# Pairs 2 to 15 of blocks in tiles of 32 rows by 64 columns, with operands gathered at half width

## The chip, the cores and the metric

The kernel runs on one core of a Trainium2 chip. The time is device microseconds of one execution: 732.87 us, the median of three runs (732.12 to 734.15). Everything is float32.

The core's engines work side by side and wait for each other by semaphores: TensorE (PE; its weight loads are shown apart as PEld), VectorE (DVE), ScalarE (ACT), GpSimd (POOL) and SyncE (SP). Here POOL does no arithmetic in the main loop: it issues indirect DMAs (gathers), whose descriptors it writes itself. SP issues plain DMAs.

## What is computed

Three layers of a compressed interaction network over x of shape (1024, 39, 64), as (sample b, field, position e):

```python
def _cin_layer(Xk, X0, W, b):
    O = W.shape[0]
    Hk, Fdim = (Xk.shape[1], X0.shape[1])
    Wr = W.reshape(O, Hk, Fdim)
    return jnp.einsum('bhe,bfe,ohf->boe', Xk, X0, Wr) + b[None, :, None]
...
for W, b in ((W0, b0), (W1, b1), (W2, b2)):
    Xk = _cin_layer(Xk, X0, W, b)
    outs.append(Xk.sum(axis=-1))
cin_output = jnp.concatenate(outs, axis=-1)
return cin_output @ fc_w.T + fc_b
```

Only a sum over e and one final number per sample are wanted. So the kernel needs, for every column (b, e), two sets of 64 values that are both sums over pairs of fields: the first layer, and a second one whose weights come from W1, W2 and fc_w. Their product, summed over e, and terms that are linear in the fields give the answer.

## The kernel before

**Blocks and pairs.** The 1024 samples are 32 blocks of 32 samples, that is 2048 columns of 64 positions each. Two blocks are a pair (0 to 15), as they share one set of short operands. In a block the 780 pairs of fields become rows of products: six chunks of 128 rows (PAIRS, NPAIR = 6), and 32 rows more, the square step, which serves four column quarters (1024 columns wide, four groups of 32 partitions).

**Gathers (POOL).** Both operands of a product are gathered by field from a table in DRAM: xd, three of them (NTAB = 3), each with the two blocks of a pair, 40 rows a block. roll(n), L178 to L181, fills rt[n % 2], five tiles of 128 x 2048, by five indirect DMAs (gather_rows, L173 to L176) with a list of rows; roll_small fills ut and vt (128 x 1024) for the pair. load(n), L166 to L171, brings block n of x into its table. Most loads are issued by SP; those of blocks 4 and 5 by POOL, in its queue between the gathers.

**Products (DVE).** product(n, c) multiplies two tiles of rt elementwise into p, 128 x 2048. The pool of p has four buffers, and the loop makes the product of step at + 4 (AHEAD) while step at is multiplied, so DVE can start one as soon as TensorE has finished the step four before it.

**Matmuls (PE).** multiply(n, c), L555 to L565, takes the 128 columns of weights wa for chunk c against the four quarters of p (512 columns), into four PSUM banks. A float32 matmul is two instructions in the profile. join(n), L567 to L596, does the square rows and the linear terms of both blocks as tiles of 32 rows by 64 columns of weights, eight of which work in the array at once: 16 for the square, 8 for the linear terms.

**Finish.** When a block's banks are complete, ACT copies one half of each with a bias (z), DVE multiplies it with the other half into g (L609), and DVE sums g over e (L620). ACT has copied the 39 field rows into g before (fields, L598).

**Order.** It is written by hand. A pair has 13 steps: six chunks, the join, six chunks. The text counts them through: pair 0 is steps 0 to 12 (6 is its join), pair 1 is 13 to 25, pair 2 begins at 26. roll(n + 2) stands behind the last product of block n, so a pair's tiles are gathered while the pair before it runs.

## Time and profile before

| | us |
|---|---|
| median of three runs | 732.87 |
| span of the profiled execution | 731.4 |
| first product matmul (L559) from the span's start | 17.1 |
| 32 blocks of six chunks, 16 joins on TensorE | L559 x1536, L579 x512, L590 x256 |

The profile was taken of one execution. Its rows give the engine, the line of the kernel, the operation, what it writes and reads (out<-in), the shape, how often, and then busy time and mean length; behind the second bar stands the idle time of the engine just before them and what ended it. A timeline row begins with the start and the length in us. "Issue" means that the profile shows nothing that was waited for. Matmuls are pipelined: an instruction's length is more than its distance from the next one.

### The profile page before, as it was taken

To read this page: it belongs to the slowest core of one execution; us is meant where nothing else is said; L and a number is where in the kernel's file an instruction comes from. 1 tells how busy PE (TensorE), PEld (TensorE's weight loads), DVE (VectorE), ACT (ScalarE), POOL (GpSimd) and SP (SyncE) were. 2 spreads that over 40 slices of the span, in tenths; PEclk is the share of its full clock that TensorE was granted. 3 is DMA by queue.
4 is the path that set the end of the run, shared out by engine and by line. 5 is a ranking of instruction groups with operands and counts; after the bars stand their busy time and mean duration, and the time that the engine had idled before them with its cause. 6 is when DMAs were issued, how large, how long until landed. Compare 5 with 4: busy or idle time off the path is not lost.

```text
span 731.4 us, 6351 instructions
## 1 busy us (share of the span) xinstructions
PE 724.7 (99%) x2375; PEld 316.1 (43%) x2375; DVE 638.3 (87%) x521; ACT 166.9 (23%) x240; POOL 397.6 (54%) x254
## 2 busy tenths in 40 slices
PE   8999999999999999999999999999999999999998
PEld 4444444444444444444444444444444444444443
DVE  6999798988889988889988889888898988889885
ACT  3332121222212222221222212222121221212222
POOL 6789886536555445754537555455654547545300
PEclk9999999999999999999999999999999999999999
DMA  8997899789575887757679675896767777565700
GB/s 268 376 337 280 315 342 356 290 307 338 232 273 231 281 336 286 270 225 285 269 288 330 223 289 219 304 348 236 268 256 274 301 287 266 224 252 236 288 0 0
DMA packets 65983, 197.24 MB, mean 270 GB/s; under 512 B 40110, under 2 KB 40179, under 8 KB 45984
## 3 DMA queue, kind: packets, MB, share of 16 engines
q0 software_dynamic: 28784, 185.56, 65.5%
q1 hardware_dynamic: 35468, 9.29, 5.5%
q10 hardware_dynamic: 1700, 1.99, 1.0%
q8 instruction: 18, 0.29, 0.1%
q14 instruction: 13, 0.11, 0.0%
HBM read 196.76 MB, written 10.60 MB: 284 GB/s over the span
## 4 chain that ended last, share of the span: by engine, by line
PE 99%; DVE 0%; DMA 0%; issue 0%; ACT 0%; DVEq 0%
PE po L559 91%; PE po L579 4%; PE po L590 2%; PE idle L279 0%; PE pv L406 0%; PE pt L487 0%; PE small L323 0%; PE pv L487 0%; PE pw L418 0%; DMA fcrow<-in_fc_w 0%; PE tr L543 0%; DVE g L609 0%; DVE pairs L526 0%; DVE sums L631 0%; ACT z L607 0%
## 5 line engine op out<-in xcount | busy, mean ns | idle before, releaser
L559 PE MATMUL po<-p,wa 128*128 128x512 f32 x1536 | 666.0, 594 | 0.0
L219 DVE TENSOR_TENSOR p<-r 128x2048 f32<-128x2048 f32 (+2 forms) x198 | 434.1, 2224 | 72.4 <-PE po L559 67.1
L559 PEld LDWEIGHTS po<-p,wa 128*128 128x128 f32 x1536 | 290.5, 190 | 371.7 <-issue 354.6
L174 POOL DMA_INDIRECT r<-xd,lists x156 | 302.3, 1938 | 267.1 <-issue 266.2
L607 ACT ACTIVATE z<-po,columns 64x512 f32<-64x512 f32 x128 | 87.3, 682 | 380.1 <-PE po L590 217.9
L609 DVE SCALAR_TENSOR_TENSOR g<-po,b0s,z 64x512 f32<-64x512 f32 x128 | 95.9, 749 | 9.3 <-ACT z L607 5.3
L602 ACT COPY g<-r 39x1024 f32<-39x1024 f32 x64 | 66.7, 1043 | 155.0 <-DVE sums L620 126.8
L620 DVE TENSOR_REDUCE sums<-g 103x16 f32<-103x1024 f32 x62 | 75.6, 1220 | 2.1
L174 POOL DMA_INDIRECT u<-xd,lists x16 | 38.9, 2432 | 7.5 <-issue 4.6
L174 POOL DMA_INDIRECT v<-xd,lists x16 | 38.5, 2403 | 4.9 <-issue 4.9
L579 PE MATMUL po<-p,wa 32*64 32x512 f32 x512 | 31.6, 600 | 0.0
L221 DVE TENSOR_TENSOR p<-u,v 128x1024 f32<-128x1024 f32 x16 | 19.5, 1218 | 0.0
L579 PEld LDWEIGHTS po<-p,wa 32*64 32x64 f32 x512 | 9.4, 131 | 20.2 <-issue 19.4
L590 PE MATMUL po<-u,wa 32*64 32x512 f32 x256 | 17.0, 587 | 0.0
L174 POOL DMA_INDIRECT r<-xh,lists x8 | 8.0, 996 | 4.8 <-DVE tmp L387 2.7
L590 PEld LDWEIGHTS po<-u,wa 32*64 32x64 f32 x256 | 5.7, 132 | 8.0 <-issue 8.0
L526 DVE TENSOR_TENSOR pairs<-both 128x2 f32<-128x2 f32 (+27 forms) x59 | 6.1, 171 | 0.2
L544 ACT COPY wa<-tr 128x128 f32<-128x128 f32 x8 | 2.1, 266 | 16.2 <-PE tr L543 16.2
L279 PE MATMUL idle<-const-float32-1.0 128*128 128x256 f32 (+1 forms) x8 | 4.0, 596 | 0.8 <-PEq L793 0.8
L543 PE MATMUL tr<-unit,pairs 128*128 128x128 f32 x8 | 2.4, 294 | 2.2 <-DVE pairs L526 2.2
L543 PEld LDWEIGHTS tr<-unit,pairs 128*128 128x128 f32 x8 | 1.2, 151 | 4.7 <-ACT pairs L524 2.7
L168 POOL DMA_DIRECT2D xd<-in_x x3 | 3.2, 1055 | 0.0
(97 smaller groups left out, 56.7 us busy)
## 6 DMA issues: line engine op xcount, KB each, us to landing
xd<-in_x SPq DMA_DIRECT2D x28, 312.0 KB
r<-xd,lists POOLq DMA_INDIRECT x156, 8.9
xd<-in_x POOLq DMA_DIRECT2D x3, 312.0 KB, 7.6
w2s<-in_w ACTq DMA_DIRECT2D x1, 624.0 KB
w1s<-in_w ACTq DMA_DIRECT2D x1, 624.0 KB
w0s<-in_w0t ACTq DMA_DIRECT2D x1, 380.2 KB
xh<-in_x ACTq DMA_DIRECT2D x2, 156.0 KB
xd<-xh SPq DMA_DIRECT2D x2, 156.0 KB
```

The source lines that it names most:

```text
L174: nc.gpsimd.indirect_dma_start(dst, None, table, bass.IndirectOffsetOnAxis(ap=lists[:, k : k + 1], axis=0))
L219: nc.vector.tensor_tensor(p[:, cols], r[:, i, cols], r[:, k, cols], ALU.mult)
L221: nc.vector.tensor_tensor(p[:, 0:SUB], ut[n // 2 % 2], vt[n // 2 % 2], ALU.mult)
L279: nc.tensor.matmul(idle[:, 0:cols], nc.const_aps.tensor(1.0, (128, 128), F32), nc.const_aps.tensor(1.0, (128, cols), F32), start=True, sto ...
L526: nc.vector.tensor_tensor(out, diagonal(a, b, sa, sb), diagonal(b, a, sb, sa), ALU.add)
L559: nc.tensor.matmul(po[n][m], wa[:, c, side : side + 2 * H], p[:, bass.ts(m, MM)], start=n % 2 == 0 and c == 0, stop=n % 2 == 1 and c == NP ...
L579: nc.tensor.matmul(dst[half * H : half * H + H], wa[rows, NPAIR, at : at + H], p[rows, bass.ts(side, MM)], start=t >= 2, stop=t < 2 and ha ...
L590: nc.tensor.matmul(dst[half : half + H], wa[rows, NPAIR + 1, H : 2 * H], ut[n // 2 % 2][rows, bass.ts(side, MM)], start=False, stop=t < 2,)
L602: nc.scalar.copy(gt[H : H + F], rt[n % 2][0:F, 0, bass.ts(m, SUB)])
L607: nc.scalar.activation(z[one], po[n][m][other], AF.Identity, bias=fc0s[other])
L609: return lambda: nc.vector.scalar_tensor_tensor(g[n][m // 2][0:H, at], po[n][m][one], b0s[one], z[one], ALU.add, ALU.mult)
L620: nc.vector.tensor_reduce(sums[:, b_at : b_at + SB], g[n][m // 2].rearrange("p (b e) -> p b e", e=E), AX.X, ALU.add,)
```

## The change

Pair 0 and pair 15 stay as they are. In pairs 1 to 14 all products and matmuls are arranged in parts t = 0 to 3:

- A part holds 32 rows of the 128 of each operand, for all four half-blocks of the pair: partitions 32 s to 32 s + 31 hold half-block s (block s // 2, half s % 2). roll_part(k, t) gathers it into half of an rt tile: five indirect DMAs of 128 x 1024, with the lists in narrow. A pair has 20 of these where it had 10 of 128 x 2048; u and v stay. The order of release is part by part: part t of pair k + 1 is gathered behind the last product of part t of pair k.
- part_product makes 2048 columns at a time: two chunks at once from 1024 columns (whole), or four or two chunks of one side, a side being one of the two 512-column quarters of the half-blocks (side, both).
- part_multiply multiplies each unit of 512 columns with 4 x 2 tiles of 32 rows by 64 columns. Row group s needs the weights of rows 32 t to 32 t + 31, so wn holds wa's rows moved to the other partitions (part_weights, twelve ACT copies during pair 0).
- A side has four banks, one for each half-block. Side 0 is complete in the middle of the last step but one of a pair and is opened again with the next pair's first step; part_finish frees the banks, and the sums follow in the next pair.
- The fields come to g by four DMAs of SP a pair (part_fields) instead of ACT copies.

The core of the diff:

```diff
+TILES = 4
+ROWS = 128 // TILES
+NPART = NBLK // 2
...
+    def roll_part(k, t):
+        table = xd[k % NTAB].rearrange("f (t c) -> (f t) c", c=SUB)
+        for i in range(NT):
+            nc.gpsimd.indirect_dma_start(
+                part(t)[:, i],
+                None,
+                table,
+                bass.IndirectOffsetOnAxis(ap=narrow[:, t, i : i + 1], axis=0),
+            )
...
+    def part_multiply(k, t, units, p, last):
+        for u, (c, side) in enumerate(units):
+            begin = open_part(k, side)
+            end = last and not any(s == side for _, s in units[u + 1 :]) and last[side]
+            for s in range(TILES):
+                rows = slice(ROWS * s, ROWS * s + ROWS)
+                w = wa[rows, c] if s == t or c == NPAIR else wn[rows, c, t]
+                for half in range(2):
+                    at = ((s + side) % 2 + half) * H
+                    nc.tensor.matmul(
+                        po[2 * k + side][s][half * H : half * H + H],
+                        w[:, at : at + H],
+                        p[rows, bass.ts(u, MM)],
+                        start=begin,
+                        stop=bool(end),
+                    )
...
+    def part_steps(k):
+        found = []
+        for t in range(TILES):
+            if t in (0, TILES - 1):
+                if t:
+                    found.append((k, t, "square", 0))
+                found += [(k, t, "side", 0), (k, t, "both", 0), (k, t, "side", 1)]
+            else:
+                found += [(k, t, "whole", at) for at in range(3)]
+        return found
+
+    WHOLE = (0, NPART - 1)
     steps = []
-    for n in range(0, NBLK, 2):
-        steps += [(n, c) for c in range(NPAIR + 1)] + [(n + 1, c) for c in range(NPAIR)]
...
+    for k in range(NPART):
+        steps += whole_steps(k) if k in WHOLE else part_steps(k)
...
-            if c == NPAIR - 1 and n + 2 < NBLK:
-                roll(n + 2)
+            k = n // 2 + 1
+            if c == NPAIR - 1 and k < NPART:
                 if n % 2 == 0:
-                    roll_small(n + 2)
-                if n < 2:
-                    load(n + 4, nc.gpsimd)
+                    roll_part(k, 0)
+                    roll_small(2 * k)
+                    roll_part(k, 1)
+                else:
+                    roll_part(k, 2)
+                    roll_part(k, 3)
+                load(n + 4, nc.gpsimd)
...
+        p[step], units_of[step] = part_product(t, kind, which)
+        done = which == (2 if kind == "whole" else 1) and k + 1 < NPART
+        if done and k + 1 not in WHOLE:
+            roll_part(k + 1, t)
+        elif done and t % 2:
+            roll(2 * k + 2 + t // 2)
+        if done and t == 1:
+            roll_small(2 * k + 2)
```

Three places of the built programs show what moves. On TensorE, the end of pair 0 and a whole pair read like this before (L559 is multiply, L579 and L590 are join):

```order
L559 MATMUL po<-p,wa 128x512
L579 MATMUL po<-p,wa 64x512 x16
L590 MATMUL po<-u_86,wa 64x512 x8
L559 MATMUL po<-p,wa 128x512 x48
L579 MATMUL po<-p,wa 64x512 x16
```

The change has this around the square of pair 1 (L633 is part_multiply, L646 the linear terms):

```order
L633 MATMUL po<-p,wa 64x512 x2
L633 MATMUL po<-p,wn 64x512 x6
L633 MATMUL po<-p,wa 64x512 x2
L633 MATMUL po<-p,wn 64x512 x2
L633 MATMUL po<-p,wa 64x512 x16
L646 MATMUL po<-u_91,wa 64x512 x8
L633 MATMUL po<-p,wn 64x512 x6
L633 MATMUL po<-p,wa 64x512 x2
```

Small tiles stand on both sides of the square, so the array keeps one shape from step 13 to the end of pair 14.

On POOL, these are the gathers of pair 1 and the first of pair 2 before (xd_69 is pair 1's table, xd_70 pair 2's, and the rows that write xd_70 are the loads of blocks 4 and 5):

```order
L174 DMA r_84<-xd_69,lists 128x2048 x5
L174 DMA u_87<-xd_69,lists 128x1024
L174 DMA v_89<-xd_69,lists 128x1024
L168 DMA xd_70<-in_x 1248x1x64
L174 DMA r_85<-xd_69,lists 128x2048 x5
L168 DMA xd_70<-in_x 1248x1x64
L174 DMA r_84<-xd_70,lists 128x2048 x5
```

In the change they are:

```order
L145 DMA r_88<-xd_69,narrow 128x1024 x5
L130 DMA u_91<-xd_69,lists 128x1024
L130 DMA v_93<-xd_69,lists 128x1024
L145 DMA r_88<-xd_69,narrow 128x1024 x5
L124 DMA xd_70<-in_x 1248x1x64
L145 DMA r_89<-xd_69,narrow 128x1024 x10
L124 DMA xd_70<-in_x 1248x1x64
L145 DMA r_88<-xd_70,narrow 128x1024 x10
```

The second load has 12 gathers of pair 1 and the first load ahead of it before the change, and 22 gathers and the first load after it. A part's gather reads rows of both blocks, so the last row shown waits for both loads, where the first gathers of pair 2 had needed one.

On DVE, from the last products of pair 1 to the finish of its side 0, the change has (p are products; those from r1_89 are of pair 1's part 3, those from r0_88 of pair 2's part 0; the rows of L697 free the banks of pair 1's side 0):

```order
L221 TENSOR_TENSOR p_909<-r1_89 128x2x2x512
L212 TENSOR_TENSOR p_943<-r1_89 128x2048
L212 TENSOR_TENSOR p_974<-r0_88 128x2048
L221 TENSOR_TENSOR p_1008<-r0_88 128x2x2x512
L697 SCALAR_TENSOR_TENSOR pairs_97<-po_611,b0s_79,z_1042 64x512
L697 SCALAR_TENSOR_TENSOR pairs_97<-po_612,b0s_79,z_1042 64x512
L697 SCALAR_TENSOR_TENSOR both_96<-po_613,b0s_79,z_1043 64x512
L697 SCALAR_TENSOR_TENSOR both_96<-po_614,b0s_79,z_1043 64x512
L212 TENSOR_TENSOR p_1052<-r0_88 128x2048
```

Before, the finish of a block stood between products too, but its banks were not opened again for six steps; here two products of the next pair stand ahead of the operations that free the banks with which that pair begins.

More of the change, by code (lines that the diff above doesn't have):

```diff
@@ L291, in cin_kernel @@
         wide = prep.tile([128, 5, NT], F32, name="wide")
-        fields_of = prep.tile([128, NT], F32, name="fields_of")
         used = [0]
@@ L379, in cin_kernel @@
             )
-        r, most, seat, far = (new() for _ in range(4))
+        r, most, far = (new() for _ in range(3))
         both_of = prep.tile([128, 2], F32, name="both_of")
@@ L687, in cin_kernel, with whole_step @@
         multiply(n, c, p[n, c], (1,))
-    for at, (n, c) in enumerate(steps[:-TAIL]):
-        if c == 0 and 2 <= n and n + 4 < NBLK:
-            load(n + 4)
+    units_of = {}
+    sums_due = []
+    def whole_step(at, n, c):
         quarters = range(BLK // MM)
@@ L716, in cin_kernel, with part_step @@
                 spread(k)
-        if at - 1 in over:
-            finish(over[at - 1])
-            fields(over[at - 1] + 1)
-        if at + AHEAD < len(steps):
-            n, c = steps[at + AHEAD]
-            if at + AHEAD <= NPAIR:
+    def part_step(k, t, kind, which):
+        tile_ = p.pop((k, t, kind, which))
+        if kind == "square":
+            part_multiply(k, t, [(NPAIR, 0), (NPAIR, 1)], tile_, None)
+            part_linear(k)
+        else:
+            last = t == TILES - 1 and kind != "whole"
+            last = last and {0: kind == "both", 1: kind == "side" and which == 1}
+            part_multiply(k, t, units_of.pop((k, t, kind, which)), tile_, last)
+        if t == TILES - 1 and kind == "both":
+            part_finish(k, 0)
+            sums_due.extend((k, 0, b) for b in range(2))
+        if t == TILES - 1 and kind == "side" and which == 1:
+            part_finish(k, 1)
+            sums_due.extend((k, 1, b) for b in range(2))
```

182 lines of the change are left out of this document (165 added, 17 removed).

## The prediction

> **What bounds the kernel now.** I read the page first (busy time, then the chain that ended last), then TensorE's timeline over one pair of blocks, then VectorE's and GpSimd's, and last the first 100 us by themselves.
>
> ```profile
> span 731.4 us, 6351 instructions
> PE 724.7 (99%) x2375; PEld 316.1 (43%) x2375; DVE 638.3 (87%) x521; ACT 166.9 (23%) x240; POOL 397.6 (54%) x254
> PE 99%; DVE 0%; DMA 0%; issue 0%; ACT 0%; DVEq 0%
> ```
>
> The chain is TensorE from end to end, so only what TensorE streams, or a new wait of TensorE, moves the time. DVE at 87% is close behind. POOL's 54% looks harmless, but it is an average over gathers that wait.
>
> ```profile
> 78.71 5.74 PE L559 MATMUL po<-p,wa 128*128 128x512 f32 x13
> 84.39 1.97 PE L579 MATMUL po<-p,wa 32*64 32x512 f32 x32
> 86.15 1.06 PE L590 MATMUL po<-u,wa 32*64 32x512 f32 x16
> 87.15 41.47 PE L559 MATMUL po<-p,wa 128*128 128x512 f32 x96
> 128.54 1.97 PE L579 MATMUL po<-p,wa 32*64 32x512 f32 x32
> ```
>
> A pair repeats every 128.54 - 84.39 = 44.15 us. A full matmul is two instructions here, and they follow each other at (5.74 - 0.59) / 12 = 0.429 us (0.59 is one instruction's own length). The small ones go eight at a time: the 32 and 16 of the join are six groups, and they take 87.15 - 84.39 = 2.76 us, 0.46 each with both changes of shape in it. So a group of eight small tiles costs about what one full instruction costs, and a pair is 96 + 6 = 102 such slots: 102 x 0.429 = 43.76 us. What is left, 0.39 us a pair, is what it costs to go from full tiles to small ones and back.
>
> **Part 1, TensorE's tiles.** A product of 2048 columns is still 8 slots, square and linear rows still 6, so a pair keeps its 102 slots. Pairs 1 to 14 (counted from 0) lose their change of shape, and one change in and out remains around them: 14 - 1 = 13 times 0.39 is **-5 us**. Bounds: if a long run of groups goes at the join's 0.46 rather than 0.429, the 14 pairs would lose 14 x 102 x 0.031 = 44 us; it cannot go below the slots, so -5 is also the best. I take -5, since 0.46 holds the two changes of shape. Weights come eight loads to a slot, as in the join. Instructions are up about sevenfold:
>
> ```profile
> q8 instruction: 18, 0.29, 0.1%
> ```
>
> That queue's share of 0.1% becomes under 1%; I cost it at nothing.
>
> **Part 2, VectorE and ScalarE.**
>
> ```profile
> L219 DVE TENSOR_TENSOR p<-r 128x2048 f32<-128x2048 f32 x188 | 424.4, 2289 | 71.6 <-PE po L559 67.1 <-DMA r<-xd,lists 4.3
> L609 DVE SCALAR_TENSOR_TENSOR g<-po,b0s,z 64x512 f32<-64x512 f32 x128 | 95.9, 749 | 9.3 <-ACT z L607 5.3
> L607 ACT ACTIVATE z<-po,columns 64x512 f32<-64x512 f32 x128 | 87.3, 682 | 380.1 <-PE po L590 217.9 <-PE po L559 157.5
> L602 ACT COPY g<-r 39x1024 f32<-39x1024 f32 x64 | 66.7, 1043 | 155.0 <-DVE sums L620 126.8 <-issue 28.2
> L620 DVE TENSOR_REDUCE sums<-g 103x16 f32<-103x1024 f32 x62 | 75.6, 1220 | 2.1
> L219 DVE TENSOR_TENSOR p<-r 128x1024 f32<-128x1024 f32 x6 | 7.2, 1218 | 0.8 <-DMA r<-xh,lists 0.7
> L219 DVE TENSOR_TENSOR p<-r 128x512 f32<-128x512 f32 x4 | 2.6, 680 | 0.0
> ```
>
> DVE's work for a pair: 12 x 2.29 + 1.22 + 8 x 0.75 + 4 x 1.22 = 39.6 us, the same kinds as before, against TensorE's 43.8. The new products read in two or four pieces. At worst a piece costs what a product of that size costs alone: 2 x 1.22 or 4 x 0.68 instead of 2.29, so 6 x 0.15 + 6 x 0.43 = 3.5 us a pair, still under 43.8; at best nothing. I take nothing. The new finish is tighter: a side's four banks close one and a half steps (5.15 us) before they are opened again, and the chain to free them is 0.68 + 4 x 0.78 = 3.8 us. It fits with about 1.3 us to spare, provided that nothing late stands ahead of it on DVE. ScalarE loses its 1.04 us copies of the fields to DMAs of SP that have half a pair to land, and gets twelve weight copies in pair 0, some 1.15 us each by the 1.04 of 1024 elements, all inside block 1's 20.6 us. The z of block 1 stand behind ten of them and end near 68.8, just before their banks are wanted (68.9): 0 to 0.5 us, I take 0. Seven small copies and one small VectorE operation in the preparation are covered:
>
> ```profile
> ACT both L464 <- PE pw L418: 3.9, 1, 3.9
> ```
>
> ScalarE waits 3.9 us at that place.
>
> **Part 3, the gathers.** Bytes stay, but a pair now has 20 + 2 gathers for POOL to write instead of 10 + 2.
>
> ```profile
> 428.02 3.41 POOL L174 DMA_INDIRECT r<-xd,lists  x1 [9.96 <-issue]
> 431.74 2.26 POOL L174 DMA_INDIRECT r<-xd,lists  x1 [0.31 <-issue]
> 434.30 0.94 POOL L174 DMA_INDIRECT r<-xd,lists  x1 [0.30 <-issue]
> 435.54 1.89 POOL L174 DMA_INDIRECT r<-xd,lists  x1 [0.31 <-issue]
> ...
> 441.18 1.90 POOL L174 DMA_INDIRECT v<-xd,lists  x1 [0.30 <-issue]
> 450.83 4.47 POOL L174 DMA_INDIRECT r<-xd,lists  x1 [7.76 <-issue]
> ```
>
> ```profile
> 430.89 2.29 DVE L219 TENSOR_TENSOR p<-r 128x2048 f32<-128x2048 f32 x1 [0.27 <-PE po L559]
> 434.33 2.30 DVE L219 TENSOR_TENSOR p<-r 128x2048 f32<-128x2048 f32 x1 [1.14 <-PE po L559]
> 447.81 8.93 DVE L219 TENSOR_TENSOR p<-r 128x2048 f32<-128x2048 f32 x4
> ```
>
> A gather's length does not follow its size. Alone it is 0.94 us and the next starts 0.30 later (1.24 in all). If a product runs when it starts, it ends 0.81 us after that product: the one of 431.74 ends at 434.00, the product at 433.18. Where products follow without a gap (the four from 447.81) it passes the first end and waits for a later one, 4.47 us in all. The Trainium skill, SBUF — State Buffer, section "SBUF: two separate sides", says that VectorE and GpSimd lock one shared port pair for a whole instruction and that the loser fully blocks, so that GpSimd cannot write descriptors; these rows agree.
>
> In the steady state there are 15 us or more between a gather and its use, so a slower POOL does no harm at first. **The start is another matter.**
>
> ```profile
> 43.13 2.47 POOL L174 DMA_INDIRECT r<-xd,lists  x1 [2.13 <-issue]
> ...
> 50.56 0.93 POOL L174 DMA_INDIRECT r<-xd,lists  x1 [0.31 <-DVE g L609]
> 51.80 12.45 POOL L174 DMA_INDIRECT u<-xd,lists  x1 [0.30 <-issue]
> 64.56 2.44 POOL L174 DMA_INDIRECT v<-xd,lists  x1 [0.30 <-issue]
> 67.00 1.06 POOL L168 DMA_DIRECT2D xd<-in_x  x1
> ...
> 82.00 1.04 POOL L168 DMA_DIRECT2D xd<-in_x  x1
> ```
>
> ```profile
> 52.35 11.09 DVE L219 TENSOR_TENSOR p<-r 128x2048 f32<-128x2048 f32 x5
> 63.89 2.29 DVE L219 TENSOR_TENSOR p<-r 128x2048 f32<-128x2048 f32 x1 [0.45 <-PE po L559]
> ```
>
> ```profile
> DMA to landing us min/median/max: 4.6/8.9/15.7
> ```
>
> In the kernel before, POOL has all of pair 1 gathered and the second load out (block 5's, 82.00) when TensorE is at step 19. Now 10 more gathers stand ahead of that load, and the first gathers of pair 2 read both blocks of their table, so they wait for it. By hand, with the durations above (4.6 us from a gather's issue to landing, 5.0 for a load, products 2.29):
> - TensorE begins pair 1 (step 13) at 84.39 - 20.6 = 63.7; step 16 is due at 74.0, step 19 at 84.3, step 23 at 97.2, step 26 (pair 2) at 107.5.
> - t0's five gathers go out from 46.9 to 52.7 beside the finish of block 0. Then come the same five products without a gap, and u waits to 63.4 as it did.
> - u, v, t1, load 4: 63.4 to 72.9. t1's third gather lands at 73.0, product 16 ends at 75.3: 1.3 us late.
> - t2 from 77.5 (products 16 and 17 shut it out) to 84.3; product 19 ends at 86.8, 1.2 late more. t3 from 86.8 to 97.1, most of it behind products 20, 21 and the square's; product 23 ends at 101.8, 2.1 late more. Load 5 ends at 98.2 and lands near 102.1.
> - t0 of pair 2 gets in after products 24 and 25: four gathers 106.2 to 110.7, landed at 114.4. Now the order on VectorE makes it worse: products 26 and 27 stand ahead of the four operations that free side 0's banks, so step 26 starts 2.3 + 2.2 + 3.1 us later, at 122.0, due at 112.1 by then: 9.9 late.
>
> In sum 14.5 us. Let a gather slip in at every second end of a gapless run (the 4.47 row), and load 5 ends near 92.8 and the same sum is 9. I take **+12 us**, nearer to the 12.45 row, which saw no end of its run. A stall this long should also cool TensorE's clock:
>
> ```profile
> 16.90:20.30 3.40, 3.40 (x7) 1.56 (x6) 3.40 (x21) 0.83 (x6) 2.90 (x2) 0.50 1.02 387
> 20.30:25.00 4.70, 4.70 (x13) 2.01 (x13) 3.93 (x6) 2.99 (x7) 1.47 (x3) 1.00 1.03 417
> ```
>
> After a thin stretch the clock (third figure from the end) stood at 0.50 for 3.4 us: 1.7 us lost. Bounds 0 to 1.7; I take **+1.7**. The Trainium skill, TensorE: Matmul & The Clock Gate, section "Part 1: The HAM clock gate", gives half the clock after one idle window of about 3.4 us; the row agrees in length.
>
> **Sum**: 731.4 - 5 + 12 + 1.7 = 740.1 us of span. The median of the runs, 732.87, lies 1.5 above this span; with it 741.6.
>
> **Rivals.** *No stall, faster.* If gathers get in at most ends of products, or landings are early, load 5 is out by about 87.5 us (t0 of pair 2 then lands by 99.8, and VectorE frees side 0 by 107.5); then only -5 counts: 727.9. For it: TensorE never waited in the start before, although u took 12.45 us. Against it: 24 POOL operations would have to pass from 46.9 to 87.5, 1.7 us each, where the trace has 14 in the 40 us from the row of 43.13 to that of 82.00. *A short stall*, where t0 alone is a little late: 2.6 to 7 us, 731 to 735. *POOL becomes the bound in every pair.* Seven gathers from 428.02 to 443.08 took 2.15 us each; 22 at that pace are 47 us, over 43.8. Against it: POOL has 8 x 0.75 + 4 x 1.22 = 10.9 us a pair beside the finish and the sums, where a gather is 1.24. If two gathers of a pair find no place, VectorE must idle 2.5 us for them, 13 times: +32 on top, 773. The skill's page on SBUF has the lock for an instruction's whole length, which speaks for this one.
>
> **Chances.** Stall in the start alone, 735 to 755: 0.40. POOL the bound, 755 and more: 0.22. Short stall: 0.15. No stall: 0.23. The range runs from 727.5 to 772: it leaves out the worse half of the POOL case, and little below. A measurement tells 0.3% from no change (2.2 us): faster 0.23, same 0.13, slower 0.64.
>
> **What would show it.** TensorE's groups of eight at 0.429 us through pairs 1 to 14 confirm part 1. Waits of VectorE's products on gathers between 70 and 120 us, a gap of TensorE near step 26 with its banks freed late, and the load at the end of t3 confirm part 3; POOL busy without a break later on means the third rival. No TensorE gap at all makes me wrong on the start, and a pace above 0.429 on part 1.

## The result, and the profile after

| | before | changed |
|---|---|---|
| median, us | 732.92 (6 runs, 732.12 to 735.41) | 812.02 (6 runs, 804.63 to 816.14) |
| ratio, 95% interval | 1 | 1.1064 [1.1023, 1.1105] |
| span of the profiled execution, us | 731.4 | 813.8 |

Medians are over all runs; ratios leave out the executions in which the chip ran in a slower state.

The change costs 79 us; 741.6 had been predicted. The page of the changed kernel (busy time, GpSimd's line in 40 slices, the chain, and the groups of products and gathers):

```profile
span 813.8 us, 25489 instructions
PE 769.2 (95%) x11783; PEld 363.0 (45%) x11783; DVE 630.1 (77%) x522; ACT 123.6 (15%) x203; POOL 655.5 (81%) x394
...
POOL 7878689888898888988889888888888889888700
...
POOL 31%; DMA 20%; PE 16%; DVE 15%; issue 15%; ACT 2%; DVEq 0%; POOLq 0%; ACTq 0%
...
L145 POOL DMA_INDIRECT r<-xd,narrow x280 | 545.8, 1949 | 93.2 <-issue 74.7
L212 DVE TENSOR_TENSOR p<-r 128x2048 f32<-128x2048 f32 x56 | 128.2, 2291 | 107.5 <-DMA r<-xd,narrow 100.7
...
L221 DVE TENSOR_TENSOR p<-r 128x2048 f32<-128x2048 f32 x28 | 64.0, 2286 | 1.9 <-DMA r<-xd,narrow 1.8
```

The chain was TensorE to 99% before; now it goes round GpSimd, the landing of its gathers, VectorE and TensorE. GpSimd is busy for 81% of the span, at 8 tenths or 9 in nearly every slice until its last gathers; the rest is mostly the 0.30 us that lies between two gathers in the rows further down. So it is full. VectorE's products have kept their length (2.29 us, in pieces or not), but now wait 100.7 us for gathers.

Most of the loss is spread over the run. The linear terms (L646) stand once in each tiled pair; this is their answer in the changed kernel, and below it in a run without the pairs' gathers (e5_no_gather, further down); 99.5 to 753.2 is from the start of the first of 14 sets to the start of the last matmul:

```profile
L646 PE MATMUL po<-u,wa x224: 587/587/588, 99.5 to 753.2; 32*64 32x512 f32 x112
```

```profile
L646 PE MATMUL po<-u,wa x224: 587/587/588, 98.9 to 671.6; 32*64 32x512 f32 x112
```

653 us in 13 periods are 50.2 us a pair, where the kernel before took 44.15; 13 x 6.1 = 79 us is the whole difference. By the starts of the sets, the first period, which holds the stall at the start, takes 56.8 us; the other twelve lie between 45.1 and 54.5 us, 49.7 in the mean, so some 67 of the 79 us are lost behind the start. Stretches of 50 us of the changed kernel (columns: length, then busy time of PE, PEld, DVE, ACT and POOL with counts, granted clock, DMA share, GB/s), and two of the kernel before:

```profile
250.00:300.00 50.00, 49.41 (x854) 21.18 (x846) 39.52 (x26) 5.47 (x8) 43.30 (x23) 0.97 0.79 261
300.00:350.00 50.00, 46.04 (x800) 22.64 (x792) 37.00 (x25) 5.46 (x8) 43.30 (x23) 0.93 0.75 255
400.00:450.00 50.00, 44.62 (x754) 20.40 (x762) 36.24 (x25) 5.46 (x8) 43.30 (x23) 0.93 0.74 248
```

```profile
150.00:200.00 50.00, 50.00 (x159) 21.63 (x158) 43.58 (x29) 12.05 (x16) 26.21 (x14) 1.00 0.76 287
200.00:250.00 50.00, 50.00 (x159) 21.76 (x158) 44.64 (x31) 11.71 (x14) 23.38 (x12) 1.00 0.75 281
```

In 50 us GpSimd gets 22 to 23 gathers done, 43.30 us busy and 0.30 after each: one pair's worth. TensorE's clock is 0.93 to 1.00 in these rows. The start of one pair, in windows of 1 us (a count takes in the instructions that are cut by the window's edges):

```profile
411.00:412.00 1.00, 0.00 (x0) 0.00 (x0) 1.00 (x1) 0.00 (x0) 1.00 (x1) 1.00 0.98 378
...
417.00:418.00 1.00, 1.00 (x8) 0.30 (x6) 0.97 (x2) 0.97 (x2) 0.70 (x2) 0.50 0.77 242
...
424.00:425.00 1.00, 1.00 (x32) 0.51 (x24) 1.00 (x1) 0.00 (x0) 0.83 (x1) 1.00 0.99 348
```

TensorE waits, then works at a granted clock of 0.50, where groups of eight follow at 0.85 us instead of 0.429, then at 1.00 again. All seven waits of over 3.5 us in these periods are followed by such a spell, and two of 1.2 and 1.6 us; the nine spells are 58 us long in all. Worked out from the starts of the matmuls, of the 85 us that the 13 periods take beyond 13 x 43.76, 44 are waits of over 1 us, some 29 are matmuls at the clock of 0.50, and some 12 the rest.

Where GpSimd loses its time is seen where its timeline and VectorE's are put side by side (start, length, engine, ...):

```profile
421.67 0.94 POOL L145 DMA_INDIRECT r<-xd,narrow  x1 [0.30 <-issue]
422.92 0.94 POOL L145 DMA_INDIRECT r<-xd,narrow  x1 [0.30 <-issue]
424.17 14.72 POOL L145 DMA_INDIRECT r<-xd,narrow  x1 [0.30 <-issue]
439.19 0.94 POOL L145 DMA_INDIRECT r<-xd,narrow  x1 [0.30 <-DVE sums L679]
```

```profile
420.59 3.09 DVE L697 SCALAR_TENSOR_TENSOR g<-po,b0s,z 64x512 f32<-64x512 f32 x4
423.61 4.47 DVE L204 TENSOR_TENSOR p<-r 128x2048 f32<-128x2048 f32 x2
428.01 1.20 DVE L679 TENSOR_REDUCE sums<-pairs 103x16 f32<-103x1024 f32 x1
429.14 2.27 DVE L207 TENSOR_TENSOR p<-r 128x2048 f32<-128x2048 f32 x1
...
435.80 2.27 DVE L204 TENSOR_TENSOR p<-r 128x2048 f32<-128x2048 f32 x1
438.00 1.20 DVE L679 TENSOR_REDUCE sums<-g 103x16 f32<-103x1024 f32 x1
```

Beside the finish (L697, which reads PSUM) gathers take 0.94 us. The one of 424.17 starts in a product and gets in nowhere while products and sums follow without a gap; it ends at 438.89, 0.82 after the last product's end at 438.07 (435.80 + 2.27). There are 13 gathers of over 8 us behind 110 us, about one a pair, the longest of 14.7; in the kernel before, none behind 110 us is over 4.5.

### The profile page after: what moved, and what is told of

It is laid out like the page before. It is cut to its first block, busy times and chain, and to the rows that moved or that the text cites. A ratio compares the mean times of both kernels' runs of the same rounds, so it can differ in the third digit from the quotient of the medians.

```text
span 813.8 us, 25489 instructions
## 1 busy us (share of the span) xinstructions
PE 769.2 (95%) x11783; PEld 363.0 (45%) x11783; DVE 630.1 (77%) x522; ACT 123.6 (15%) x203; POOL 655.5 (81%) x394
## 3 DMA queue, kind: packets, MB, share of 16 engines
q8 instruction: 92, 1.51, 0.7%
## 4 chain that ended last, share of the span: by engine, by line
POOL 31%; DMA 20%; PE 16%; DVE 15%; issue 15%; ACT 2%; DVEq 0%; POOLq 0%; ACTq 0%
POOL r L145 28%; DMA r<-xd,narrow 18%; PE po L633 9%; PE po L571 5%; DVE p L204 3%; DVE p L212 2%; DVE sums L679 2%; DVE g L697 2%; DVE p L221 2%; ACT wn L611 1%; POOL v L130 1%; DVE pairs L697 1%; DMA b0s<-in_b 1%; POOL r L130 1%; POOL u L130 1%
## 5 line engine op out<-in xcount | busy, mean ns | idle before, releaser
L633 PE MATMUL po<-p,wa 32*64 32x512 f32 x3136 | 637.6, 603 | 31.4 <-DVE pairs L697 31.4
L633 PE MATMUL po<-p,wn 32*64 32x512 f32 x8064 | 624.5, 604 | 5.7 <-DVE p L204 3.0
L145 POOL DMA_INDIRECT r<-xd,narrow x280 | 545.8, 1949 | 93.2 <-issue 74.7
L633 PEld LDWEIGHTS po<-p,wn 32*64 32x64 f32 x8064 | 274.4, 135 | 275.2 <-issue 230.8
L633 PEld LDWEIGHTS po<-p,wa 32*64 32x64 f32 x3136 | 198.5, 135 | 103.7 <-issue 62.1
L212 DVE TENSOR_TENSOR p<-r 128x2048 f32<-128x2048 f32 x56 | 128.2, 2291 | 107.5 <-DMA r<-xd,narrow 100.7
L204 DVE TENSOR_TENSOR p<-r 128x2048 f32<-128x2048 f32 x56 | 126.5, 2280 | 31.8 <-DMA r<-xd,narrow 24.9
L571 PE MATMUL po<-p,wa 128*128 128x512 f32 x192 | 85.8, 602 | 0.5 <-DVE p L192 0.5
L207 DVE TENSOR_TENSOR p<-r 128x2048 f32<-128x2048 f32 x28 | 63.8, 2280 | 15.8 <-DMA r<-xd,narrow 15.8
L221 DVE TENSOR_TENSOR p<-r 128x2048 f32<-128x2048 f32 x28 | 64.0, 2286 | 1.9 <-DMA r<-xd,narrow 1.8
L192 DVE TENSOR_TENSOR p<-r 128x2048 f32<-128x2048 f32 (+2 forms) x30 | 54.7, 1855 | 8.9 <-DMA r<-xd,lists 4.5
L697 DVE SCALAR_TENSOR_TENSOR g<-po,b0s,z 64x512 f32<-64x512 f32 x72 | 53.9, 749 | 6.7 <-ACT z L695 4.6
L571 PEld LDWEIGHTS po<-p,wa 128*128 128x128 f32 x192 | 36.0, 193 | 46.9 <-issue 39.7
L130 POOL DMA_INDIRECT r<-xd,lists x16 | 32.9, 2055 | 5.7 <-issue 4.6
L646 PE MATMUL po<-u,wa 32*64 32x512 f32 x224 | 24.3, 587 | 0.0
L697 DVE SCALAR_TENSOR_TENSOR both<-po,b0s,z 64x512 f32<-64x512 f32 x28 | 21.0, 749 | 0.9
L697 DVE SCALAR_TENSOR_TENSOR pairs<-po,b0s,z 64x512 f32<-64x512 f32 x28 | 20.9, 746 | 0.5
```

The lines of the kernel that those rows point to most:

```text
L130: nc.gpsimd.indirect_dma_start(dst, None, table, bass.IndirectOffsetOnAxis(ap=lists[:, k : k + 1], axis=0))
L145: nc.gpsimd.indirect_dma_start(part(t)[:, i], None, table, bass.IndirectOffsetOnAxis(ap=narrow[:, t, i : i + 1], axis=0),)
L192: nc.vector.tensor_tensor(p[:, cols], r[:, i, cols], r[:, k, cols], ALU.mult)
L204: nc.vector.tensor_tensor(out, one, r[:, 1:3], ALU.mult)
L207: nc.vector.tensor_tensor(out, r[:, 0:4:3], one, ALU.mult)
L212: nc.vector.tensor_tensor(p.rearrange("p (i k c) -> p i k c", i=2, k=2), r[:, 0:4:3, cols].unsqueeze(2).to_broadcast(shape), r[:, 1:3, col ...
```

## The experiments

Theories: **A**, GpSimd, shut out by VectorE's products, cannot do 22 gathers in 43.8 us. **B**, something else in the arrangement (small tiles, products in pieces, hand-over of banks). **C**, bytes and landings. Later **D**, TensorE's small matmuls are stopped by the gathers themselves, and **F**, the place of the sums. Ratios are to the kernel before, with 95% intervals.

| run | gathers a pair | us | ratio |
|---|---|---|---|
| e1_split_before | 22, full tiles | 836.4 | 1.140 [1.135, 1.145] |
| e2_wide | 12 wide | 799.1 | 1.085 [1.082, 1.089] |
| e3_half_products | 22 | 1039.8 | 1.416 [1.409, 1.422] |
| e4_half_bytes | 22 | 903.7 | 1.234 [1.225, 1.242] |
| e5_no_gather | 2 | 732.6 | 0.999 [0.996, 1.002] |
| e6_wide_row128 | 12 wide | 780.6 | 1.063 [1.059, 1.066] |
| e7_row128 | 22 | 813.7 | 1.107 [1.101, 1.112] |
| e8_nop_before | 12 wide, full tiles | 733.9 | 1.001 [0.999, 1.002] |
| e9_half_products_row128 | 22 | 734.3 | 1.001 [0.999, 1.003] |
| e10_part0_sp | 17 | 783.5 | 1.066 [1.063, 1.068] |
| e11_early_loads | 22 | 804.4 | 1.095 [1.091, 1.099] |
| e12_sums_with_finish | 22 | 822.2 | 1.119 [1.116, 1.123] |
| e13_wide_row128_sums | 12 wide | 760.4 | 1.036 [1.033, 1.038] |
| e14_ten_plain | 12 | 1062.7 | 1.449 [1.446, 1.452] |
| e15_fifteen | 15 | 876.9 | 1.197 [1.193, 1.201] |
| e16_fifteen_spread | 15 | 862.2 | 1.176 [1.174, 1.178] |
| e17_spread | 22 | 805.9 | 1.099 [1.095, 1.103] |
| e18_seventeen | 17 | 806.7 | 1.094 [1.089, 1.099] |

**e1_split_before: the number of gathers, without the rest of the change**

```diff
+            if 2 <= n < NBLK - 2:
+                for t in range(2):
+                    nc.gpsimd.indirect_dma_start(
+                        rt[n % 2][:, i, t * SUB : (t + 1) * SUB],
+                        None,
+                        table.rearrange("f (t c) -> (f t) c", c=SUB),
+                        bass.IndirectOffsetOnAxis(ap=lists2[:, t, k : k + 1], axis=0),
+                    )
...
```

> The kernel before, with every gather of pairs 1 to 14 cut into two of 128x1024: 22 gathers a pair instead of 12, the same bytes, the same full-height matmuls and products. Theory A (GpSimd has no room for 22 gathers beside VectorE's products, some 50 us of gathering a pair against TensorE's 44): 785 to 820 us. Rival B (the small tiles, the products in pieces or the tight hand-over of the banks made the changed kernel slow): none of that is in here, so 733 +- 3. Rival C (the bytes and their landing): bytes are the same, 733 to 740.

836.4 us, above A's range and far from B's and C's. On its page POOL is at 81% again, a gather at 2.08 us:

```profile
PE 757.4 (91%) x2375; PEld 320.4 (38%) x2375; DVE 635.2 (76%) x525; ACT 166.8 (20%) x240; POOL 678.6 (81%) x394
L184 POOL DMA_INDIRECT r<-xd,lists x280 | 582.4, 2080 | 87.6 <-issue 79.9
```

Ten gathers more a pair, same bytes, full tiles: that alone is enough for the whole loss. Behind 110 us 23 of its gathers take over 8 us, the longest 14.8, although its sums stand in the finish as in the kernel before.

**e2_wide, e6_wide_row128: the change with the old number of gathers**

```diff
-        if done and k + 1 not in WHOLE:
-            roll_part(k + 1, t)
-        elif done and t % 2:
+        if done and t % 2:
             roll(2 * k + 2 + t // 2)
```

> The changed kernel with ten gathers of 128x2048 a pair instead of twenty of 128x1024 (the operands hold whole blocks' rows, so the output is not the reference's); small tiles, products, banks and field transfers as in the changed kernel. Theory A: 12 gathers a pair fit, so only the saved changes of tile shape are left, 726 to 735 us, and GpSimd's busy time falls from 655 us to about 400. Rival B: 800 or more. Rival C: bytes are the same, so 800 or more too, unless the size of a row matters.

799.1 us: A's number missed by 64, and B's and C's "800 or more" is nearer. But its sign of A came: POOL is at 442 us instead of 655, so GpSimd is not the bound here, and the chain is TensorE at 91%. Something else slows the tiles once GpSimd is free. In e6 the two matmuls of 64 columns became one of 128:

```diff
-                for half in range(2):
-                    at = ((s + side) % 2 + half) * H
...
+                at = (s + side) % 2 * H
...
```

> Ten wide gathers a pair as in e2_wide, and in the parts one matmul of 32 rows by 128 columns of weights instead of two of 64: half of TensorE's instructions, the same stream. New theory D (while gathers load the DMA engines fully, TensorE gets only some 8 instructions in 0.25 to 0.95 us, which stops a tiled unit of 32 instructions but not a full one of 4): half the instructions, so at most half of the loss of 70 us that e2_wide shows against 728: 727 to 762. Rival B (anything else of the arrangement: banks, products in pieces, field transfers): about 799 as e2_wide.

780.6: 18.5 less, but not down into the range. So half of TensorE's instructions is worth something here (D), and what is left is not the number of gathers; e13 comes back to it.

**e3_half_products, e9_half_products_row128: free GpSimd from the products**

```diff
-            out = p.rearrange("p (k c) -> p k c", k=2)
+            out = p[:, 0:SUB].rearrange("p (k c) -> p k c", k=2)
...
-                        p[rows, bass.ts(u, MM)],
+                        p[rows, bass.ts(u % 2, MM)],
```

> The changed kernel with products of 1024 columns instead of 2048 (the second half of each product is left out, and the matmuls read the first half twice; 22 narrow gathers a pair stay). Theory A in its sharper form, that a gather is held up by VectorE's products: products shut GpSimd out for some 15 us a pair instead of 28, so 22 gathers take 22 x 1.24 + at most 15 = 42 us and fit: 728 to 748 us, with a start stall at most. If instead 22 gathers by themselves take 2.25 us each, whatever VectorE does: about 812. Rival B: about 812, or less by what the products in pieces cost. Rival C: about 812.

1039.8 us, the opposite of what A had promised, and it showed the second mechanism. Gathers were fast (1.02 us in the mean), and TensorE was the chain. Four stretches of 3 us:

```profile
200.00:203.00 3.00, 3.00 (x65) 1.70 (x57) 1.87 (x2) 0.00 (x0) 0.91 (x1) 1.00 0.00 0
203.00:206.00 3.00, 3.00 (x43) 1.09 (x30) 0.00 (x0) 0.00 (x0) 2.08 (x4) 1.00 0.64 180
206.00:209.00 3.00, 2.65 (x17) 0.42 (x9) 0.00 (x0) 0.00 (x0) 1.85 (x2) 1.00 0.99 358
209.00:212.00 3.00, 2.86 (x52) 1.59 (x59) 2.00 (x3) 1.47 (x3) 0.00 (x0) 1.00 0.89 339
```

The count behind PE falls from 65 to 17 while GpSimd issues five gathers in a row and the DMA engines fill up, with the clock still at 1.00, and recovers when the gathers are out. No wait that would explain it is shown in that time. VectorE does nothing meanwhile (0.00 in the two middle rows), so no product holds up the next gather. e9 is the same kernel with matmuls of 128 columns:

> e3_half_products (products of 1024 columns, the matmuls read them twice; 22 narrow gathers a pair) with matmuls of 32 rows by 128 columns, so half of TensorE's instructions. Theory D (32 matmuls and weight loads a unit are stopped while gathers load the DMA engines, 16 are not): the loss of 300 us in e3_half_products goes for the most part, 730 to 780. If it was something else in the bunched gathers (the half products, the landings): 950 to 1040.

734.3 us, from 1039.8. Both halves of the theory are in this one page:

```profile
PE 726.3 (99%) x6183; PEld 340.9 (46%) x6183; DVE 459.3 (63%) x522; ACT 123.7 (17%) x203; POOL 470.3 (64%) x394
PE 99%; DVE 1%; POOL 0%; issue 0%; ACT 0%; DVEq 0%
L145 POOL DMA_INDIRECT r<-xd,narrow x280 | 384.2, 1372 | 160.6 <-issue 73.7
```

The 22 narrow gathers of the change, its bytes, its field transfers, its banks are all there, and TensorE is the chain to 99% again. Only the products are half as long (half of each is left out), and a matmul instruction does twice the columns. The second alone gains nothing (e7, further down: 813.7 us, a gather at 1.96); with the first a gather falls to 1.37 us and the loss is gone. Half products also leave VectorE itself more room (63% busy), and the run does not part the two; but in the changed kernel it is VectorE, at 77%, that waits for the gathers. So A is right for the changed kernel, neither B without gathers (e5) nor C explains the loss, and D is real where gathers come in bursts.

**e4_half_bytes**

```diff
-        table = xd[k % NTAB].rearrange("f (t c) -> (f t) c", c=SUB)
+        table = xd[k % NTAB].rearrange("f (t c) -> (f t) c", c=MM)
...
-                part(t)[:, i],
+                part(t)[:, i, 0:MM],
```

> The changed kernel with its twenty gathers at 128x512 instead of 128x1024 (half of every operand row is left out of the gather, and the products read what an earlier gather left there). Theory A (the number of gathers counts, not their bytes): 800 to 815 us, gathers of the same mean length of 1.95 us. Rival C (bytes, or the time to land): the landing wait of VectorE shrinks, 740 to 775. Rival B: about 812.

903.7, outside every range. Half of the bytes made it slower, the opposite of what C says. Its chain is TensorE to 95%, its gathers 1.66 us: like e3, it lets gathers through faster and pays on TensorE. Why these gathers are faster than full ones was not traced.

**e5_no_gather**

```diff
-        if done and k + 1 not in WHOLE:
-            roll_part(k + 1, t)
-        elif done and t % 2:
+        if done and k + 1 in WHOLE and t % 2:
```

> The changed kernel without the twenty narrow gathers in pairs 2 to 14 (they are left out, so products there use pair 1's rows; u and v are still gathered, small tiles and field transfers stay). If small tiles by themselves are as fast as full ones (prediction, part 1), and only gathers slow the kernel, through GpSimd or through the DMA engines: 726 to 732 us with a start stall of at most 10 more. If small tiles are slow without any DMA beside them: 780 or more.

732.6 (729.6 to 737.8), within what was written. The row of L646 shown above gives 44.1 us a pair in the mean; by the starts of the sets the first period takes 46.2 us (pair 1's gathers are still there before it) and all later ones 43.8, 102 slots of 0.429 us. Small tiles, products in pieces, the tight hand-over of banks and the fields by DMA cost nothing when no gathers come.

**e7_row128: is D the bound in the change?** The edit of e6 in the changed kernel:

> The changed kernel with one matmul of 32 rows by 128 columns instead of two of 64, the 22 narrow gathers a pair as they are; the same output. If TensorE's instruction supply (D) alone set the 812 us: 735 to 765. If GpSimd (A) alone would already set it, as e1_split_before with 836 us at full tiles says: 800 to 836, no better than before by more than 2%.

813.7, the same as 812.0. With half of the instructions GpSimd is as full (647.6 us) and nothing is gained: in the changed kernel D adds nothing that shows beside A.

**e8_nop_before**

```diff
+            if 2 <= n < NBLK - 2:
+                for _ in range(28):
+                    nc.tensor.nop(nofuse=True)
```

> The kernel before with 28 empty instructions on TensorE behind each 512-column matmul of blocks 2 to 29, so that it issues 32 instructions a unit as the changed kernel does, with full tiles, 12 wide gathers a pair and the same computation. Theory D in its plain form, that any TensorE instruction counts: 770 to 830 us. Rival E (only the small matmuls and weight loads themselves are slowed beside the DMA, by their reads of SBUF or by being started and recorded, not by their number in the queue): 733 to 740.

733.9, but this tells nothing: the page counts 18 packets of the instruction queue, as before the edit, so the empty instructions were not in the program that ran.

**e11_early_loads: the start stall**

```diff
-            for k in (2, 3):
+            for k in (2, 3, 4, 5):
                 load(k)
...
-                load(n + 4, nc.gpsimd)
```

> The changed kernel with the loads of blocks 4 and 5 issued by SyncE at step 0 instead of by GpSimd between the gathers. Theory A with GpSimd full from pair 1 to the end: its pause of 5.9 us before pair 2 and two issues of 1.4 us go, and all that is behind moves up: 8 to 9 us less, 800 to 807. If the start stall is a cost of its own, as the prediction had it (12 us and a cool clock): 797 to 802. If GpSimd is not the bound: 812, or within 4 of it.

804.4, 7.6 less: GpSimd's pause before pair 2 is gone. The interval of its ratio, 800 to 805 us for a kernel before of 733, reaches into A's range and that of the start stall, so the run does not tell them apart.

**e12, e13, e17: the place of the sums**

```diff
             part_finish(k, 0)
-            sums_due.extend((k, 0, b) for b in range(2))
+            for b in range(2):
+                part_sum(k, 0, b)
```

> The changed kernel with each side's two sums right behind its four finishing operations on VectorE instead of one behind each of the next pair's products; all else as in the changed kernel, the same output. Theory F (in the changed kernel the sums stand without a gap between products, and GpSimd gets in nowhere in that run, 8 to 15 us a pair; beside the finish they would give it 4.8 us more of free time): the long gathers of 8 us and more go, GpSimd needs less DVE idling, 775 to 800 us; 22 gathers still do not fit. If only the number of gathers counts, wherever the sums stand: 804 to 816.

> e6_wide_row128 (12 wide gathers a pair, matmuls of 32 by 128; 780.6 us) with the sums right behind the finish. Theory F: its loss of 52 us against 728 came from the run of products and sums that shuts GpSimd out for 8 to 12 us and makes ten gathers come in one burst; with the sums moved 728 to 745. If the burst comes from where rt is released and not from the sums: 770 to 785.

e12: 822.2, 10 us more where F had a gain. The long gathers did not go: 13 are over 8 us, the longest of 15.8, and the mean is 2.02 us (1.95 in the changed kernel). Moving the sums to the finish leaves the products behind it without a gap. e13: 760.4, between the two ranges and 20 less than e6, with pairs of 45.7 us; its longest gather behind 110 us is 7.2 us, where e6 has 13 over 8. There the sums' place is part of what e6 lost. Of what is left, 1.9 us a pair over the 43.8, the view of waits has 16.4 us in all, 1.3 a pair, in which TensorE's weight loads wait for the finish of side 1 (g), which now stands behind side 0's sums (8.1 us in e6); the rest was not traced. e17 puts one sum behind every second product in the middle of the next pair (and its edit moves the fields' DMAs to part 3, not shown):

```diff
-        elif sums_due and not (len(step) == 4 and step[1] == TILES - 1):
+        elif sums_due and (len(step) == 2 or part_steps(step[0]).index(step) in (3, 5, 7, 9)):
```

> The changed kernel with the sums apart as in e16_fifteen_spread, all else as it is: 22 narrow gathers a pair, matmuls of 32 by 64. e12_sums_with_finish moved them into the hand-over of the banks, which cost TensorE 20.7 us there and spoilt it as a test. Theory F: 770 to 800. If the number of gathers alone counts: 804 to 816.

805.9: just inside the range for "number alone", and its interval touches that of the changed kernel. One gather over 8 us is left (9.2), yet the mean only falls to 1.89: the time that the long gathers lost is lost by the others in smaller pieces. So with 22 gathers the sums' place is worth some 6 us, and under 12 by the outer ends of the intervals. The text on record blames the hand-over of the banks for e12 by 20.7 us; that figure does not show it, since TensorE's wait of L633 for the finish in `pairs` is 31.4 us in the changed kernel and 20.7 in e12:

```profile
PE po L633 <- DVE pairs L697: 31.4, 8, 8.8
```

```profile
PE po L633 <- DVE pairs L697: 20.7, 8, 8.7
```

(The view groups waits: who waits, for what; us in all, count, the longest.) What does grow in e12 is the weight loads' wait for side 1's finish (g), from 6.0 to 26.7 us, while theirs for `pairs` falls from 44.9 to 35.3. What makes e12 slower stays open.

**Attempts at a version that beats both: e10, e14, e15, e16, e18.** In parts 0 to 2 a tile's 32 rows are one to three runs of consecutive fields in each half-block, so plain DMAs can bring it:

```diff
+                        nc.sync.dma_start(
+                            part(t)[ROWS * s + row : ROWS * s + row + n, i],
+                            xd[k % NTAB][
+                                s // 2 * FT + f : s // 2 * FT + f + n,
+                                s % 2 * SUB : s % 2 * SUB + SUB,
+                            ],
+                        )
...
```

> An attempt at a version that beats both: matmuls of 32 by 128 as in e7_row128; part 0's five gathers a pair replaced by 32 plain DMAs of SyncE (a tile's 32 rows are one or two runs of fields in each half-block), so GpSimd has 17 a pair; the loads of blocks 4 and 5 issued at the start by SyncE. The same output. Theory A (some 18 gathers have room beside VectorE's products in 43.8 us): 727 to 740. If 17 are still too many, at the 2.25 us a gather of the changed kernel's pairs they take 38 us, which would fit; by the lock alone, with runs of products that shut GpSimd out for 15 us, 745 to 790.

783.5, in the range for runs of products that shut GpSimd out: most pairs alternate between 44.2 us and 50 to 54. The longest gathers are 19 us, through the run of products and sums after the finish; a burst follows, and lands late:

```profile
320.08 19.18 POOL L161 DMA_INDIRECT r<-xd,narrow  x1 [0.30 <-issue]
339.56 0.94 POOL L161 DMA_INDIRECT r<-xd,narrow  x1 [0.30 <-issue]
```

> The second attempt at a version that beats both: matmuls of 32 by 128; ten of the twenty narrow tiles a pair brought by plain DMAs (part 0 and two tiles of part 1 on SyncE, 48 DMAs; three tiles of part 2 on ScalarE's queue, 24), so GpSimd has 12 gathers a pair; loads of blocks 4 and 5 at the start; sums behind the finish. The same output. If gathers, instruction count and the place of the sums are all there is: 727 to 733, with a pair every 43.8 us. If ScalarE's DMAs delay its part of the finish, or SyncE's 48 DMAs at 0.63 us each (30 us a pair) come late: 735 to 770.

1062.7, outside both ranges: the plain DMAs in ScalarE's queue hold back the z of the finish, as the rival said, at about nine times its price (329 us over the kernel before, where it had at most 37):

```profile
ACT z L717 <- DMA r<-xd: 788.3, 13, 70.7
```

> e10_part0_sp with two tiles of part 1 brought by SyncE as well (48 plain DMAs a pair, some 30 us of its time at 0.63 us each), so 15 gathers a pair on GpSimd, and with the linear terms' matmuls at 32 by 128 too, so that no change of tile shape is left in pairs 1 to 14. The same output. e10 had every second pair at 44.2 us and the others at 51 to 54. If two gathers fewer are enough: every pair at 43.8, 727 to 734 us. If the run of products and sums that shuts GpSimd out for 19 us still makes gathers late: 745 to 780.

> e15_fifteen with the sums apart: one of the four behind every second product in the middle of the next pair, instead of one behind each of its first four. The same output. Theory F (the gapless run sets how long GpSimd is shut out): the longest gather falls from 19 us to 12 or less, every pair at 43.8, 727 to 734. If the place of the sums does not matter: the same time as e15_fifteen.

876.9 and 862.2, far above every range but "the same time as e15_fifteen". In e16 no gather behind 110 us is longer than 5.0 us, GpSimd is at 47%, and yet only 15 us are won: the wait has moved to SyncE. Its queue in e16 (start, length, then what it issues):

```profile
408.92 20.15 SPq L158 DMA_DIRECT2D r<-xd  x32
430.13 7.58 SPq L124 DMA_DIRECT2D xd<-in_x  x2
437.82 19.69 SPq L158 DMA_DIRECT2D r<-xd  x16
457.62 0.83 SPq L684 DMA_DIRECT2D pairs<-xd  x1
```

It never pauses, and the loads of the coming pair stand in it.

> e10_part0_sp (17 gathers a pair on GpSimd, 32 plain DMAs on SyncE, matmuls of 32 by 128) with the sums apart as in e17_spread, the linear terms at 32 by 128, and the loads of the coming blocks issued by ScalarE, so that SyncE keeps 20 to 25 us of DMAs a pair where e16_fifteen_spread kept it busy without a break. The same output. If GpSimd shut out for 19 us was what made every second pair of e10 late: all pairs at 43.8, 727 to 737. If 17 gathers are too many in any order: 755 to 785, as e10 (783.5).

806.7, above both ranges. Eight of its 13 periods take 44.6 us, but the others up to 60.6, and the way into the first tiled pair takes 82.5 where the changed kernel needs 57.6. GpSimd is at 52% and SyncE pauses, but SyncE's 32 DMAs now take 28 us instead of 20, and a gather lands 11.5 us after its issue (median; 6.7 in the changed kernel). So 17 gathers were not tried under clean conditions, and no version here that does the whole computation beats the kernel before.

## Why the prediction was wrong

**Part 1 was right.** Groups of eight at 0.429 us, 43.8 us a pair without gathers (e5). The saving of 0.39 us a pair is there in the later periods of e5 and invisible behind the rest; e5's total, 732.6, does not show it; about half of it goes in e5's first period (46.2 us), and where the rest goes was not traced.

**Part 2 was right for the products (2.28 to 2.29 us in each form) and the finish**, as long as gathers come in time.

**Part 3, the start, came, its number partly by luck.** Step 26 started at 120.76 after a TensorE gap of 9.4 us, where 122.0 and 9.9 had been worked out, behind a late load 5 (out at 96.2, foreseen 98.2) and late banks as described. But u took 5.7 us instead of the 12.45 on which the choice of +12 rested, pair 2's first product began at 115.44 (its operands had been foreseen at 114.4), and step 26 followed it by 5.3 us instead of 7.6: these errors cancel. Removing the cause of it gives back 7.6 us (e11), of 12 + 1.7 foreseen.

**The step that failed is the one sentence on the steady state**: "In the steady state there are 15 us or more between a gather and its use, so a slower POOL does no harm at first." Slack between a gather and its use hides a late gather once. It does not help an engine whose 22 gathers need 22 x (1.95 + 0.30) = 49.5 us in a period of 43.8. The order should have been: first the engine's load over a pair, then the slack. The load could be read from before: in the two stretches of 50 us shown above GpSimd was busy 49.60 us with 26 instructions, 1.91 each and 0.30 after it; 22 of 2.21 are 48.6 us, an estimate that takes their length as unchanged. The prediction had even written 47 us for the rival, and then gave it 0.22.

**Why the rival was argued down.** "POOL has 8 x 0.75 + 4 x 1.22 = 10.9 us a pair beside the finish and the sums, where a gather is 1.24." The 6 us beside the finish are real (the 0.94 rows at 421.67). The 4.9 us beside the sums are not: in this order the sums stand gapless between products, and GpSimd gets in nowhere in that run (the 14.72 row). In the kernel before, a block's sums stood among its finishing operations. But their place is not the whole answer: e1 and e12, with the sums at the finish, take 836.4 and 822.2 us, and e17 gains some 6 us, so 22 gathers do not fit with that room either.

**The rival's price was also too low**: 2.5 us a pair, for two gathers without a place, 32 in all. Behind the start it was 49.7 - 43.8 = 5.9 us a pair. About a third of the loss is the clock: put at 0 to 1.7 us, once, for the start, it went to 0.50 in nine places and cost some 29 us by the working above, and the rival's price had none of it. That VectorE, once late, makes up by products without a gap, which shut GpSimd out again, is argued here and not shown.

**The cost put at nothing, TensorE's instructions** (2375 matmuls became 11783, five times and not seven), was right for the changed kernel (e7) and would have been wrong next: with the number of gathers of before, the tiles of 64 columns cost 18.5 us more than those of 128 (e2 against e6).

The Trainium skill, SBUF — State Buffer, section "SBUF: two separate sides", has VectorE and GpSimd lock a shared port for whole instructions. The runs agree where products are halved: a gather falls from 1.95 to 1.37 us (e9). But they show more than one instruction's wait: the gather of 424.17 stays out through five products and the three sums between them.

## What to carry to other kernels

Before a change adds instructions to an engine that another one shuts out, divide its busy time, with the gaps between its instructions, by their number in a steady stretch, and multiply by the new number: if that exceeds the bound's period, no slack saves it. Count the price of the bound engine's waits with the cool clock behind each. What such an engine needs are pauses of the other one, so look at where the other's instructions follow without a gap, not at which of them are harmless alone. And when an experiment frees one resource and the time gets worse, look for what the freed engine now does in bursts.

## What was not expected of the hardware

**TensorE's small matmuls stop while gathers are issued into busy DMA engines.** This table is worked out from windows of 1 us between 150 and 710 us, at a granted clock over 0.95, sorted by GpSimd's busy time and the DMA share in the window; it gives the mean count behind PE. A count takes in the instructions cut by the window's edges, so 29.6 is the full pace: 8 in 0.429 us are 18.6 a us, and each is 0.59 us long.

| | GpSimd 0.6 us or more, DMA 0.95 or more | GpSimd idle, DMA 0.95 or more | DMA under 0.3, GpSimd idle |
|---|---|---|---|
| e3_half_products (64 columns) | 7.4 | 21.9 | 29.6 |
| e2_wide (64 columns) | 23.5 | 29.4 | 29.8 |
| e6_wide_row128 (128 columns) | 14.6 | 11.0 | 14.8 |

By their starts, the first row is 4.2, 15.7 and 18.7 matmuls a us. With 16 matmul instructions and 16 weight loads for 512 columns TensorE is slowed, with half of them it is not (the 11.0 holds low windows that lie together once a pair, where its banks come late). In the changed kernel, whose gathers are spread out, it is 16.9 a us by starts in the first column's windows, and e2_wide has 14.6. In a stopped stretch instructions come by twos to fours, 0.25 to 0.95 us apart, and the profile shows nothing that they wait for. The Trainium skill, Runtime: NRT & Kernel Launch, section "Instruction fetch mechanics", says that instructions come in blocks of 16 KiB (256 of them) by a DMA queue of their own, and that this is mostly hidden. The packets agree in size (92 for 1.51 MB, 16 KB each). But late blocks would be expected to stop TensorE once in 256 instructions, not every few, and few stops have a packet near them: of 848 pauses over 0.25 us between 200 and 700 us of e3_half_products, 131 have one within a microsecond, no more than the packets' number makes by chance. Whether it is the fetch, something at the issue of each instruction, or the tiles' reads stays open; e8_nop_before was meant to tell and could not.

**A gather can be shut out for 19 us** (e10, the row of 320.08), through seven products and four sums, although it takes 0.94 us alone, and although a sum in the finish leaves it room: in e1_split_before a gather from 411.79 takes 0.94 us, with a sum on VectorE from 412.27 on. Why the sums between products do not let it in stays open.
